# Graph kernel on one core: the second phase's inputs set up inside the last hidden products, adjacency's combinations moved from graph 0's attention to graph 1's, queries' combinations reordered

## Chip, cores and metric

The kernel runs on one core of one Trainium2 chip, in float32. The metric is the device time in microseconds, median of the timed runs. TensorE (PE) multiplies, VectorE (DVE) and ScalarE (ACT) do the elementwise work, GpSimd (POOL) does a little of it and issues stores, SyncE (SP) issues loads. Each engine works through its own instructions in program order and waits on semaphores for the others.

## The reference, cut to what matters

```python
# x: 16 graphs (B) of 1024 nodes (N) by 256 channels (C); adj: 1024 x 1024
h = max(layernorm(x), 0)
# layer 0: a graph product makes the queries, then attention of 4 heads
diff = c_adj[:, None, :] - c_adj[:, :, None]        # c_adj: mean over channels
A_s  = symmetrised abs(abs(sigmoid(diff) - 0.5) - 0.5) * 2
q    = relu(einsum('bcn,bnm->bcm', h^T, adj * A_s) * para)
k, v = split(h @ kv_w)
x    = x + softmax(q k^T * scale) v
# layer 1: aggregation with the normalised adjacency, two dense layers
h     = max(layernorm(x), 0)
A     = adj + I;  deg = column sums + row sums - diagonal of A
A_hat = A * rsqrt(deg)[:, None] * rsqrt(deg)[None, :]
y     = (A_hat @ h) @ W1.T + b1                     # 256 -> 512
y     = relu(batchnorm(y))                          # statistics over all graphs and nodes
out   = batchnorm(y @ W2.T + b2)                    # 512 -> 256
x     = x + out
```

Batch normalisation over all 16 graphs divides the kernel into two phases: no graph can be normalised before the hidden products of all of them exist.

## The kernel before

The **first phase** (`layers`) takes the graphs in turn. Attention of graph b (`attention`, 16 steps of scores, exponentials, sums and value products) is woven with a stream of other products, `background(b)`: queries (L155 by `queries`), keys and values of graph b + 1, and aggregation (`aggregate`, product pa) and hidden products (`hidden`, product py) of graph b - 1. The order is written out by hand: generators yield after each piece of about 1.71 us of TensorE, and `weave` lets side generators go on by one slot for each piece of the main one. An action given to `soon` is emitted after the next piece.

Products of 2 x 2 blocks are done with seven multiplications instead of eight, so sums and differences of blocks are needed ahead: `combine` (L415) for the normalised nodes, `take` (L455, DVE L457) for the weighted adjacency `w` in `queries`, and for A itself, once for all graphs, inside `degrees` (L209). There the transposed adjacency is loaded in eight tiles (tag `adj`, 3 buffers, shared with the loads of `adj` for the weights, L165), ScalarE sums its rows (L228), DVE takes the diagonal and adds the identity (L234 to L236), GpSimd forms the four differences (L241 to L244), and three DMAs on GpSimd's queue store the seven blocks to the DRAM tensor `aht_d` (L246 to L248). `aggregate` loads them for each graph (L600). `degrees` runs in graph 0's attention, as a side of graph 1's plain queries; `dinv`, the root of the degrees, is needed by the second norm of each graph (`shift`, L284).

`queries` runs seven products i of two pieces each. After piece 2 (`midway` of i = 1) it does `take(0,2,0,0)` and `take(0,2,0,1)`, which overwrite the right-hand blocks that product i = 2 reads. `first`, `second` and so on empty the PSUM bank of their product.

In graph b's attention the second norm of graph b - 1 (`normed`) is woven with queries from piece 9 on. Its `scale` is an rsqrt of two GpSimd instructions (L81, L82), its `shift` is on DVE. `combine("b", ...)` follows at its end.

After graph 15's attention `aggregate(15)` and `hidden(15)` run alone. Each hidden product is biased by ScalarE (L677), stored to `y1_d` by GpSimd (L678), and its statistics are taken by DVE (L681, L683).

The **second phase** (`second`) has pools of its own, opened after those of the first are closed. It loads W2 (L1078), computes the normalisation's scale and shift from the statistics, in two halves (`affine`), forms W2's combinations on GpSimd (L1091 to L1094), loads the first four inputs (`load_y`, L1101), applies relu on ScalarE (L1107) and the combinations of inputs (`combine_1` to `combine_3`), and then takes the graphs in turn: seven products m1 to m7 each (L1145), while `ahead_of` prepares the next graph's inputs. After the last graph come the second normalisation, transposes (L1263), the residual (L1269) and the output.

Of the kernel before, what the change touches and what calls it, by code (L numbers as in the profile page):

```python
# [17 lines left out]
P = 128  # L18
# [5 lines left out]
def gnn_two_layers_kernel(  # L24
# [59 lines left out]
    def layers(shifted):  # L84
# [7 lines left out]
        st = ExitStack()  # L92
        big = st.enter_context(tc.tile_pool(name=f"big_{kind}", bufs=1))
        py = st.enter_context(tc.tile_pool(name=f"py_{kind}", bufs=4))
# [4 lines left out]
        p4 = st.enter_context(tc.tile_pool(name=f"p4_{kind}", bufs=4))  # L99
        ps_sc = st.enter_context(tc.tile_pool(name=f"ps_sc_{kind}", bufs=2, space=PSUM))  # L100
# [75 lines left out]
        kvw = big.tile([P, CC, 2 * C], F32, name="kvw")  # L176
# [27 lines left out]
        deg_sm = big.tile([P, 7, NT], F32, name="deg")  # L204
        w1 = big.tile([P, CC, H1], F32, name="w1")
        dbc = big.tile([P, N], F32, name="dbc")
        row, diag, col, col_2, deg, tmp_deg, dinv = (deg_sm[:, i, :] for i in range(7))

        def degrees():  # L209

            nc.sync.dma_start(out=w1, in_=w1_t.rearrange("(k p) j -> p k j", p=P))
            nc.vector.tensor_reduce(row, rows.rearrange("p q t -> p t q"), AX.X, ALU.add)
            HT, HB = NT // 2, FB // 2
            for t in range(HT):
                for part, sums in enumerate((col, col_2)):
# [8 lines left out]
                    for n in range(2):  # L226
                        u = t + n * HT
                        nc.scalar.activation(  # L228
                            a[:, n], a[:, n], AF.Copy, accum_out=sums[:, u : u + 1]
                        )  # L230
                        if part == t * P // HB:
                            blk = a[:, n, n, t * P % HB : t * P % HB + P]
                            db = py.tile([P, P], F32, tag="y", name=f"db_{u}")
                            nc.vector.tensor_mul(db, blk, ident)  # L234
                            nc.vector.tensor_reduce(diag[:, u : u + 1], db, AX.X, ALU.add)
                            nc.vector.tensor_add(blk, blk, ident)  # L236
# [13 lines left out]
            nc.vector.tensor_add(col, col, col_2)  # L250
            nc.vector.tensor_add(deg, col, row)
            nc.vector.tensor_sub(deg, deg, diag)
            rsqrt(dinv, deg, 1.0, tmp_deg)
# [169 lines left out]
        def queries(b):  # L423
# [35 lines left out]
            def first(m):  # L459
                nc.scalar.copy(c12, m)  # L460
                nc.scalar.copy(c21, m)
                nc.vector.tensor_sub(a11, s1, a11)

            def second(m):
                add(c11, m, c12)
                nc.vector.tensor_sub(a12, a12, a11)
                soon(lambda: finish(0, 0))
# [871 lines left out]
```

## Time and profile before

| what | value |
|---|---|
| timed runs, median (range) | 2699.11 us (2698.63 to 2700.57) |
| span of the profiled execution | 2697.0 us (timed 2698.89) |
| first score product | 60.6 us |
| TensorE idle before the second phase's first product | 10.76 us, until 2418.80 |
| second phase's products | 2418.80 to 2614.9 us |
| last output transfers | 53 us, until 2680 us |

A row of waits reads: the engine and line that waited, the one that ended the wait, total us, how often, longest. A row of a timeline reads: start in us, duration, engine, line, operation, written and read tiles, shapes, count, and in brackets the idle time before and what ended it. In the kernel's names `au_f` is a tile of the transposed adjacency, `two` and `one` are the differences, `sc` scores, `p` exponentials, `o` value products.

### The profile page before, as it was taken

The numbers are of one execution on the slowest core, as the hardware profiler recorded it, in microseconds if no ns is written. First come the engines' busy times: TensorE is split into PE (matmuls) and PEld (weight loads), VectorE is DVE, ScalarE is ACT, GpSimd is POOL, SyncE is SP. The second block draws the span as 40 slices with busy tenths as digits, with TensorE's granted clock in tenths as the row PEclk, the third lists the DMA queues.
The fourth block names the chain that finished last, engine by engine and source line by source line (L and its number), as shares of the span: only waits on it lengthen the run. The fifth ranks groups of instructions, "written<-read, shape, count | busy, mean of one in ns | idle before, by whom it ended". The sixth has DMA issues, their size and how long they took to land.

```text
span 2697.0 us, 32235 instructions
## 1 busy us (share of the span) xinstructions
PE 2579.3 (96%) x11882; PEld 953.2 (35%) x11882; DVE 1742.1 (65%) x2777; ACT 1338.3 (50%) x1953; POOL 547.1 (20%) x624
## 2 busy tenths in 40 slices
PE   8689999999999999999999999999999999989994
PEld 3233333333333333333333333333333333324443
DVE  5457676666767575766666676757576665547674
ACT  5545463636454554546363645545453634335543
POOL 1341101111111111111111111111111111026653
PEclk9899999999999999999999999999999999999997
DMA  4331424242423324242424232231424233345559
GB/s 164 127 124 51 172 79 168 79 172 74 140 96 109 126 62 159 70 168 83 169 79 157 82 132 100 98 133 63 164 79 168 80 132 114 113 187 199 191 189 358
DMA packets 133606, 351.39 MB, mean 130 GB/s; under 512 B 17856, under 2 KB 38848, under 8 KB 127296
## 3 DMA queue, kind: packets, MB, share of 16 engines
q1 hardware_dynamic: 107968, 274.25, 29.0%
q0 software_dynamic: 25472, 75.00, 8.5%
q8 instruction: 96, 1.57, 0.2%
q14 instruction: 70, 0.57, 0.1%
HBM read 274.47 MB, written 74.71 MB: 129 GB/s over the span
## 4 chain that ended last, share of the span: by engine, by line
PE 79%; DVE 7%; ACT 4%; DMA 4%; issue 3%; POOL 2%; SPq 0%; POOLq 0%; DVEq 0%; ACTq 0%
PE sc L827 16%; PE o L868 16%; PE pa L155 13%; PE pg L155 9%; PE py L155 8%; PE m_f L1145 7%; PE pk L155 4%; PE pv L155 2%; PE sums L885 2%; DMA out_dram<-xo_f 2%; DVE acc L857 2%; ACT w L395 1%; PE htp L353 1%; ACT w L403 1%; DVE q L484 1%
## 5 line engine op out<-in xcount | busy, mean ns | idle before, releaser
L835 ACT ACTIVATE p<-sc 128x1024 f32<-128x1024 f32 x512 | 495.2, 1019 | 644.0 <-PE sc L827 643.1
L857 DVE TENSOR_TENSOR acc<-acc,p 128x1024 f32<-128x1024 f32 x384 | 470.9, 1226 | 154.7 <-ACT p L835 134.7
L827 PE MATMUL sc<-q,k 64*128 64x512 f32 x2048 | 514.2, 621 | 29.0 <-ACT p L835 29.0
L868 PE MATMUL o<-p,v 128*64 128x512 f32 x2048 | 497.2, 606 | 0.0
L155 PE MATMUL pg<-w,h_a 128*64 128x512 f32 x1600 | 359.7, 595 | 3.9 <-ACT k L567 2.1
L155 PE MATMUL pa<-aht,h_b 128*64 128x512 f32 x1536 | 343.5, 592 | 0.0
L827 PEld LDWEIGHTS sc<-q,k 64*128 64x128 f32 x2048 | 177.6, 187 | 351.1 <-issue 291.7
L888 POOL DMA_DIRECT2D sums_d<-row x64 | 37.2, 582 | 1051.0 <-ACT row L887 1051.0
L155 PE MATMUL py<-at,w 128*64 128x512 f32 x1024 | 230.3, 592 | 0.0
L868 PEld LDWEIGHTS o<-p,v 128*64 128x64 f32 x2048 | 124.7, 136 | 286.7 <-issue 284.4
L382 DVE SCALAR_TENSOR_TENSOR w<-w,adj 128x1024 f32<-128x1024 f32 x128 | 156.7, 1224 | 101.8 <-ACT w L403 97.8
L155 PEld LDWEIGHTS pg<-w,h_a 128*64 128x64 f32 x1600 | 115.8, 138 | 233.5 <-issue 212.4
L155 PEld LDWEIGHTS pa<-aht,h_b 128*64 128x64 f32 x1536 | 110.4, 137 | 213.2 <-issue 197.5
L677 ACT ACTIVATE y<-py,vec 128x512 f32<-128x512 f32 x128 | 87.6, 684 | 169.2 <-PE py L155 112.2
L395 ACT ACTIVATE w<-cbc,csum 128x512 f32<-128x512 f32 x256 | 170.0, 715 | 0.0
L854 DVE TENSOR_TENSOR acc<-p,p 128x1024 f32<-128x1024 f32 x64 | 78.9, 1233 | 116.2 <-ACT p L835 116.2
L678 POOL DMA_DIRECT2D y_d<-y x128 | 69.9, 546 | 343.9 <-ACT y L677 336.8
L403 ACT ACTIVATE w<-w 128x1024 f32<-128x1024 f32 x128 | 135.0, 1055 | 1.8
L457 DVE TENSOR_TENSOR w<-w,w 128x1024 f32<-128x1024 f32 x112 | 131.4, 1214 | 0.0
L155 PE MATMUL pv<-kvw,ht 128*64 128x256 f32 x1024 | 119.2, 380 | 10.6 <-DVE v L584 10.6
L893 POOL DMA_DIRECT2D inv<-sums_d x128 | 98.2, 770 | 137.6 <-DMA sums_d<-row 93.1
L681 DVE BATCH_NORM_STATS2 stats<-y 128x6 f32<-128x512 f32 x128 | 85.7, 687 | 61.5 <-ACT y L677 59.6
(155 smaller groups left out, 2840.5 us busy)
## 6 DMA issues: line engine op xcount, KB each, us to landing
aht<-aht_d SPq DMA_DIRECT2D x224, 512.0 KB, 6.1
adj<-in_adj_dram SPq DMA_DIRECT2D x128, 512.0 KB, 4.4
y_d<-y POOLq DMA_DIRECT2D x128, 256.0 KB, 2.6
yin_f<-y_d SPq DMA_DIRECT2D x32, 1024.0 KB, 6.3
x<-in_x_dram SPq DMA_DIRECT2D x32, 512.0 KB, 5.1
para<-in_para_dram SPq DMA_DIRECT2D x64, 256.0 KB, 3.9
x_d<-x POOLq DMA_DIRECT2D x16, 1024.0 KB, 10.2
xo_f<-x_d SPq DMA_DIRECT2D x32, 512.0 KB, 8.9
```

Source lines behind the costliest of these rows:

```text
L155: nc.tensor.matmul(dst[r], left[:, r], right, start=start, stop=stop)
L382: nc.vector.scalar_tensor_tensor(w, w, 1.0, a, op0=ALU.add, op1=ALU.mult)
L395: nc.scalar.activation(w[:, t, :], cbc[:, q * FB : (q + 1) * FB], AF.Abs, bias=csum[:, th * TH + t : th * TH + t + 1], scale=-1.0,)
L403: nc.scalar.activation(made[i], made[i], AF.Tanh, scale=-0.5 / C)
L457: nc.vector.tensor_sub(block(i)[part], block(x)[part], block(y)[part])
L677: nc.scalar.activation(y, made, AF.Identity, bias=b1[:, j : j + 1])
L827: nc.tensor.matmul(sc[:, e, :], ks[b][k][r, m * P : (m + 1) * P], qs[b][k][r, f * FB : (f + 1) * FB], start=True, stop=True,)
L835: nc.scalar.activation(pr, sc, AF.Exp)
L857: nc.vector.tensor_add(self.acc, self.acc, pr)
L868: nc.tensor.matmul(self.o[r, :], vs[b][k][:, m, r], pr[:, e, :], start=(m == 0), stop=(m == NT - 1),)
L893: nc.gpsimd.dma_start(out=self.inv[:, :, e], in_=sums_d[u][e].rearrange("(j q) -> q j", q=P))
L1145: nc.tensor.matmul(made, left[:, j, :], right[:, j, :], start=(j == 0), stop=(j == JH - 1))
```

## The change

Three things are done.

1. **Second phase.** `second` becomes a generator, created before `aggregate(15)` and advanced by `hidden(15)`: before the first hidden product it issues the loads of W2 and of the first two inputs and the combinations of W2; after pieces 3 to 7 it goes on with the first half of the scales, two relus, and at the end the rest of graph 0's preparation. To make room, the attention's pools (`p4`, `ps_sc`) lie on the right side and are closed after attention, and `io`, `wp` and `ps` of the second phase take their place; W2 takes the place of `kvw`, its combinations that of `dbc`, and graph 0's difference tiles that of `both`. `hidden(15)` orders its parts by j alone. The loads of inputs 2 and 3 come after graph 0's preparation.
2. **Adjacency.** `degrees` keeps loads, sums and diagonals, with loads of whole rows, and no longer stores. A new `graph()` loads the transposed adjacency again, in the old form, and does combinations and stores; it is a side of graph 1's background (4 slots in the first weave, 12 in the queries' weave, ahead of the norm). The identity is now added by GpSimd. One more key-value product precedes `columns_of(dinv)`.
3. **Queries and combine.** `take(0,2,0,0)` moves to `first`, the subtraction of a11 from `first` to `second`. `combine("b", ...)` moves from the norm's end into `aggregate`, after its first piece.

```diff
         def degrees():
             nc.sync.dma_start(out=w1, in_=w1_t.rearrange("(k p) j -> p k j", p=P))
             nc.vector.tensor_reduce(row, rows.rearrange("p q t -> p t q"), AX.X, ALU.add)
+            for t in range(NT):
+                a = load_adj_t(t, "at")
+                yield 0.0
+                blk = a[:, t * P : (t + 1) * P]
+                nc.scalar.activation(a, a, AF.Copy, accum_out=col[:, t : t + 1])
+                db = p1.tile([P, P], F32, tag="s1", name=f"db_{t}")
+                nc.vector.tensor_mul(db, blk, ident)
+                nc.vector.tensor_reduce(diag[:, t : t + 1], db, AX.X, ALU.add)
+                yield 0.0
...
+        def graph():
             HT, HB = NT // 2, FB // 2
             for t in range(HT):
-                for part, sums in enumerate((col, col_2)):
+                for part in range(2):
...
                     for n in range(2):
-                        u = t + n * HT
-                        nc.scalar.activation(
-                            a[:, n], a[:, n], AF.Copy, accum_out=sums[:, u : u + 1]
-                        )
                         if part == t * P // HB:
                             blk = a[:, n, n, t * P % HB : t * P % HB + P]
-                            db = py.tile([P, P], F32, tag="y", name=f"db_{u}")
-                            nc.vector.tensor_mul(db, blk, ident)
-                            nc.vector.tensor_reduce(diag[:, u : u + 1], db, AX.X, ALU.add)
-                            nc.vector.tensor_add(blk, blk, ident)
+                            nc.gpsimd.tensor_add(blk, blk, ident)
...
             def first(m):
                 nc.scalar.copy(c12, m)
                 nc.scalar.copy(c21, m)
-                nc.vector.tensor_sub(a11, s1, a11)
+                take(0, 2, 0, 0)
 
             def second(m):
                 add(c11, m, c12)
+                nc.vector.tensor_sub(a11, s1, a11)
                 nc.vector.tensor_sub(a12, a12, a11)
...
-                    (a12, 1, ((0, 2, 0, 0), (0, 2, 0, 1)), second),
+                    (a12, 1, ((0, 2, 0, 1),), second),
...
                     if th == NP // 2 - 1:
                         after(made)
+                    elif i == 0:
+                        combine("b", b, nc.vector)
...
             if b == B - 1:
-                parts.sort(key=lambda part: part[1] + 1.5 * part[0])
-            for g, j in parts:
+                parts.sort(key=lambda part: part[1])
+                next(turns[0])
+            for n, (g, j) in enumerate(parts):
...
                 soon(stats)
+                if b == B - 1 and n >= len(parts) // 2 - 1:
+                    soon(lambda: next(turns[0]))
...
-                yield from weave(islice(products, 4), (0, islice(w, 4)))
-                yield from weave(queries(b + 1), (0, double(w)), (9, islice(norm, 5)))
+                combined = graph() if b == 1 else iter(())
+                yield from weave(islice(products, 4), (0, islice(w, 4)), (0, islice(combined, 4)))
+                yield from weave(
+                    queries(b + 1), (0, double(w)), (0, combined), (9, islice(norm, 5))
+                )
...
-            for i in range(4):
-                load_y(i)
-            for i in range(2):
-                relu(i, 0)
+            load_y(0)
+            load_y(1)
+            yield
+            affine(0)
+            yield
+            yield
+            relu(0, 0, (0,))
+            yield
+            relu(0, 0, (1,))
+            yield
+            relu(1, 0)
             combine_1(0, nc.vector)
-            for i in (1, 0):
+            affine(1)
+            for i in (0, 1):
                 relu(i, 1)
             combine_2(0, nc.vector)
             combine_3(0)
+            load_y(2)
+            load_y(3)
+            yield
```

## The prediction

> **What bounds the kernel now.** I read the page's busy shares and slices first, then TensorE's waits over the whole span, then the busy time of the stretches where they lie, and last the queues that feed those stretches.
>
> ```profile
> PE 2579.3 (96%) x11882; PEld 953.2 (35%) x11882; DVE 1742.1 (65%) x2777; ACT 1338.3 (50%) x1953; POOL 547.1 (20%) x624
> ...
> PE   8689999999999999999999999999999999989994
> ```
>
> TensorE is busy 96%. The slices (67 us each) show less in three places: slices 1 to 3, slice 36 (2360 to 2427 us) and the output tail. TensorE's waits say who holds it up:
>
> ```profile
> PE sc L827 <- ACT p L835: 29.0, 5, 14.0
> PE m_f L1145 <- ACT yin_f L1107: 10.8, 1, 10.8
> PE pv L155 <- DVE v L584: 10.6, 14, 0.8
> PE pg L155 <- DVE w L457: 9.3, 13, 0.7
> ```
>
> Three of these four lie where the change works: 28.5 of the 29.0 us fall between 84 and 166 us (graph 0's attention), the 10.8 us are the passage into the second phase, the 9.3 us are one wait of 0.7 us in each of 13 graphs. Graph 0's attention by stretches (time, then busy us of PE, PEld, DVE, ACT, POOL, granted clock, DMA share, GB/s):
>
> ```profile
> 84.00:114.00 30.00, 14.76 (x58) 4.01 (x54) 10.15 (x30) 15.78 (x34) 14.29 (x19) 0.80 0.54 184
> 114.00:129.00 15.00, 9.20 (x32) 2.89 (x32) 2.98 (x3) 9.29 (x20) 8.67 (x13) 0.84 0.43 132
> ...
> 165.00:186.00 21.00, 21.00 (x100) 7.29 (x100) 13.91 (x22) 7.55 (x11) 15.25 (x18) 1.00 0.43 137
> ```
>
> No engine is full there, so it is a chain of waits. The chain that ended last names it: a combined adjacency block goes out, and only then the next one comes in.
>
> ```profile
> 91.31 4.29 DMA aht_d<-au_f
> 96.35 3.44 DMA au_f<-in_adj_t_dram
> 102.73 5.10 DMA aht_d<-au_f
> 108.50 3.50 DMA au_f<-in_adj_t_dram
> ```
>
> One turn takes 108.5 - 96.35 = 12.2 us. ScalarE, which must sum each block, stands before it (27.0 us over seven waits), and the exponentials queued behind the sum are what scores wait for.
>
> [...] eight score matmuls took 3.79 us after the idle 14.0 us and 1.99 us otherwise, so each long stall costs 1.8 us more. [...] the subtraction L243 takes 0.71 to 1.79 us. [...]
>
> **Part 1, adjacency's combinations leave graph 0.** From the starts of the score groups (92.68, 114.87, 129.20, 140.49, 153.69, 164.74) less the work between them at full clock (scores 1.92, outputs 1.87, sums 0.86, transposes 0.5, 1.71 for each product piece): 22.2 - 8.1, 14.3 - 7.2, 11.3 - 7.8, 13.2 - 5.5, 11.0 - 8.1, that is 14.1 + 7.1 + 3.5 + 7.7 + 2.9; and 4.9 before 92.68. Sum lost: **40.2 us**, slow clock included. The sums, the diagonals and the loads of the transposed adjacency stay (eight tiles of 512 KB), so ScalarE keeps its work; what goes is that a tile is held until its store lands. ScalarE's queue ahead of the exponentials that the 14.0 us wait is for, from 79.9: four key copies (0.57), five pairs of abs (1.33), five tanh (1.06), three sums (1.25), four relus of 0.77: 21 us, to 101; two tiles that land late add an estimated 1.6 and 2.9 (each behind a DVE product that waits for the previous sum). So scores start again at about 106.4 instead of 114.9, 5.6 us after the work ends, plus 1.8 of clock; the first 4.9 stay, and one wait of 1.3 remains. Left: 13.6. **Gain 26.6** (bounds: 34 if the loads are never late, 12 if each is).
>
> **Part 2, they go into graph 1.** No wait on TensorE is there now except 0.7 and 0.8. GpSimd then has per block four subtractions (means of L241 to L244 0.83 + 0.84 + 1.11 + 0.98) and three store issues (0.82 + 0.71 + 0.58): 5.9 us. The additions of the identity (before 0.28 on DVE) come to GpSimd, two for each of four blocks: between half of the 0.83 us of a double-sized row and all of it; I take 0.55. Eight blocks: 47.0 + 4.4 = 51.4. In its queue lie also one unit's sums (issue 0.57, wait 2.6, two issues of 1.55: 4.7) and two rsqrt of the first graph's second norm (1.10 + 2.06 and 0.57 + 1.33, mean 2.5). It starts after an inv load that now ends at 224.1. Without a wait for data the second rsqrt ends at 224.1 + 51.4 + 4.7 + 5.0 = 285.2. The first loads also wait: blocks and weights' adjacency share three buffers, four weights' tiles still have to come, so blocks 1 and 2 each wait for the store of the one before. Block 1: store issued near 229, landed 232.4, loaded 236.4, while GpSimd was free at 231: 5.4 lost; block 2 likewise 4.8. End: 295.4. Who waits: on DVE the scale of the norm (L284, now at 272.22), and behind it in order the unit's output, two accumulations and the copies of v.
>
> ```profile
> 268.92 0.13 DVE L284 TENSOR_TENSOR lnsm_b<-lnsm_b,deg 128x4 f32<-128x4 f32 x1
> ...
> 272.22 0.16 DVE L284 TENSOR_TENSOR lnsm_b<-lnsm_b,deg 128x4 f32<-128x4 f32 x1 [0.33 <-POOL lnsm_b L82]
> ...
> 277.34 1.41 DVE L584 COPY v<-pv 128x256 f32<-128x256 f32 x4
> ```
>
> The pv product that needs these copies starts at 278.2, 5.8 us after L284's second start. With 285.2 it starts at 291, with 295.4 at 301: 13 to 23 us later; I take the middle, 18, and 2 for the clock: **loss 20**. Stalls on the delayed adjacency tiles for w (estimated 5 us near 247) lie within this, since GpSimd's chain runs on meanwhile. The gather's first loads need the last store, estimated landed at 292 to 297; pa begins after pv, so this is about even. SP's para loads behind a waiting block have six pieces of slack.
>
> **Part 3, queries.** The first of the two subtractions L457 (1.22 us) moves ahead by one product, in the place of a 0.69 us subtraction that goes to `second`, both on DVE. The product waiting for it needs it at 239.3 in graph 1 and gets it at 240.0; moved, it ends near 233, eight pieces of work earlier than needed. DVE stands 0.5 us later ahead of accumulations that wait for ScalarE anyway (0.59). **Gain 9.3** (bounds 5 and 9.3). `combine` of the second norm (two of 0.69 us) moves a piece later, ahead of its first reader; nothing waited for it, 0.
>
> **Part 4, the passage.** Now the last py ends at 2408.0 (2418.80 less 10.76) and graph 1's first product starts at 2433.57: 25.6 us for 12.0 of work (28 records of 0.43). New, from T = 2408.0: w2, its combinations, the first inputs and half of the scales are ready; the weights' combinations (4 x 0.72) wait only for dbc's last reader at 2395.8. m1 runs to T + 1.7. Then the relu of input 1 (1.5 after the y at T + 0.9 and one relu), combine_1 (1.23): m5 at T + 4.5 to 6.2; the second scales at T + 5.0, relu 0.75 each: m2 to T + 8.0; relus to T + 8.1, combine_2 to T + 9.3: m6 to 11.1, then m7, m3, m4 without a wait to 16.2, and 1.8 for the clock: 18.0. **Gain 7.6** (bounds 0, if the loads don't come early, and 10). At the second py piece, at[1] is scaled at 2395.77, as the piece begins at 2395.85: 0. The tail follows unchanged, since it starts with the last statistics.
>
> **Sum** on the profiled span: 2697.0 - 26.6 + 20 - 9.3 - 7.6 = 2673.5. The timed runs stand 2.1 us above the span (2699.1), so **2675.6**.
>
> **Rivals.** (a) Graph 1 hides it all: GpSimd is busy 2 of 50 us in 200 to 250 and 10 of 50 after. Against it: DVE queues behind GpSimd's rsqrt. Loss 2 instead of 20: 2657.6. (b) Graph 0 stays bound by ScalarE's sums behind late loads: gain 12 instead of 26.6: 2690.2. For it: the 27.0 us wait is on loads; against: the chain shows stores ahead of the loads. (c) Slower: every block, not two, waits for the store before it, as nearly all did in graph 0. With 12.2 us a turn the eighth block is loaded at 218.7 + 7 x 12.2 = 304.1, combined at 313.4, rsqrt and the unit's sums bring 320, the product 326: 48 late, 2 for the clock, loss 50: 2705.6. It decides from a turn of about 11.5 us on all eight. Against: after four blocks no weights' tile is left in the three buffers. (d) The passage's loads come no earlier: 2683.2.
>
> **Chances.** Forecast (with d) 0.54, (a) 0.22, (b) 0.13, (c) 0.11. Range 2655 to 2693: from just past (a) to past (b), leaving (c) out. About 0.2% (5.4 us) is what a measurement can tell from no change: faster means under 2693.7. Faster: forecast and (a) whole, most of (b): 0.85; same 0.07 from the ends of (b) and (c); slower 0.08.
>
> **What would show it.** In graph 0: waits of scores on ScalarE below 10 us, none of SP for a store. In graph 1: GpSimd's blocks from 224 to some 290, DVE L284 waiting over 8 us for POOL, pv or pg idle near 280. L457 gone from TensorE's waits. At the passage m_f starting within 0.2 us of the last py, then gaps of 2 to 3 us. Wrong if graph 1 shows no idle TensorE, or graph 0 still more than 20 us.

## The result and the profile after

The changed kernel takes **2681.2 us** (median; 2680.35 to 2681.5) where the kernel before took 2699.09 in the same comparison (2698.63 to 2700.57). The ratio is 0.9932, 95% interval 0.9915 to 0.9949: faster by 17.9 us. The forecast was 2675.6 in a range of 2655 to 2693. The time lies inside, 5.6 us above the middle. The kernel before was timed again beside each later group of kernels, with medians of 2699.97, 2699.52 and 2700.44; the changed kernel was not, so a difference of a later kernel to it is good to about 1.4 us.

The two profiled spans, 2697.0 and 2678.6 us, can be cut at events that both kernels have. The last column is the forecast for the same stretch.

| stretch (us) | before | after | change | forecast |
|---|---|---|---|---|
| start to graph 0's first scores | 60.6 | 60.7 | +0.1 | 0 |
| graph 0: first scores to the 24 key products (pk) in a row that begin graph 1's attention | 156.6 | 131.2 | -25.5 | -26.6 |
| graph 1: those products to the first pa | 68.3 | 96.8 | +28.5 | +20 |
| first pa to the last py (queries in graphs 2 to 13) | 2122.5 | 2111.4 | -11.1 | -9.3 |
| passage: last py to graph 1's first m_f | 25.5 | 16.6 | -8.9 | -7.6 |
| second phase's products, then output | 263.4 | 261.9 | -1.6 | 0 |

So every term had the right sign, and graph 1 lost 8.5 us more than was put down for it. All that graph 0 gained was lost again in graph 1; what the kernel won in all is the queries, the passage and 1.6 us at the end.

Products are named as in the kernel: pg is a product of the queries, pk and pv of keys and values, m_f of the second phase, `sums` adds up the exponentials. Line numbers are those of the kernel that is shown, so L155 of the kernel before is L158 here.

**Page.** Busy times and TensorE's slices (67 us each) of the kernel after:

```profile
PE 2577.6 (96%) x11882; PEld 953.2 (36%) x11882; DVE 1744.0 (65%) x2768; ACT 1336.8 (50%) x1937; POOL 552.8 (21%) x632
...
PE   8897899999999999999999999999999999999994
```

Before, this row began with 8689. The 6 in slice 2 (67 to 134 us, graph 0) has become an 8, and the two 9s in slices 4 and 5 (201 to 335 us) have become a 7 and an 8: the hole has moved from graph 0 to graph 1. The 8 in slice 36 is now a 9.

**TensorE's waits** of the kernel after (total us, how often, longest):

```profile
PE pv L158 <- DVE v L591: 15.7, 14, 5.8
PE sc L841 <- ACT p L849: 11.3, 5, 5.4
PE pv L158 <- DVE q L497: 8.4, 1, 8.4
...
PE pg L158 <- DVE w L388: 4.9, 1, 4.9
```

Scores waiting for exponentials fell from 29.0 to 11.3 us. The 10.8 us of m_f for its input are gone, and short waits stand there (0.5, 1.6 and 1.5 us, shown below). The thirteen waits of pg for the subtraction in the queries are gone too. New are three single waits: 8.4 us and 5.8 us of pv, 4.9 us of pg. All three lie in graph 1, as the next views show.

**Stretches** of the kernel after (us, busy us of each engine, granted clock, DMA share, GB/s); the first two are shown of the kernel before too:

```profile
84.00:114.00 30.00, 21.85 (x92) 6.60 (x88) 10.99 (x28) 22.78 (x43) 6.52 (x7) 0.94 0.54 158
114.00:129.00 15.00, 12.23 (x54) 3.74 (x52) 8.56 (x14) 11.03 (x18) 0.00 (x0) 1.00 0.35 106
...
240.00:290.00 50.00, 32.88 (x154) 13.37 (x152) 25.23 (x51) 12.12 (x18) 31.03 (x44) 0.76 0.70 243
```

In 84 to 114 us TensorE works 21.9 instead of 14.8 us, at a clock of 0.94 instead of 0.80. The last line is the new weak stretch: 32.9 of 50 us, at a clock of 0.76, while GpSimd works 31 us of it.

**The hole in graph 1**, TensorE's timeline of the kernel after (the first line is the longest wait left of graph 0's stall):

```profile
105.47 3.62 PE L841 MATMUL sc<-q,k 64*128 64x512 f32 x8 [5.39 <-ACT p L849]
...
227.75 3.21 PE L158 MATMUL pg<-w,h_a 128*64 128x512 f32 x8 [4.89 <-DVE w L388]
...
253.02 3.78 PE L841 MATMUL sc<-q,k 64*128 64x512 f32 x8 [2.96 <-ACT p L849]
...
270.42 3.68 PE L158 MATMUL pv<-kvw_f,ht 128*64 128x256 f32 x16 [8.39 <-DVE q L497]
...
279.87 3.42 PE L158 MATMUL pv<-kvw_f,ht 128*64 128x256 f32 x16 [5.77 <-DVE v L591]
```

The last four lines are graph 1's: 22.0 us of waits, and each of the rows behind them takes 1.3 to 1.8 us longer than the same row elsewhere. What DVE did at those times, its timeline (kernel after):

```profile
226.19 1.50 DVE L388 SCALAR_TENSOR_TENSOR w<-w,adj 128x1024 f32<-128x1024 f32 x1 [7.00 <-DMA adj<-in_adj_dram]
...
265.78 0.42 DVE L290 TENSOR_TENSOR lnsm_b<-lnsm_b,deg 128x4 f32<-128x4 f32 x1 [7.56 <-POOL lnsm_b L82]
...
269.68 0.68 DVE L497 TENSOR_TENSOR q<-pg,q 128x512 f32<-128x512 f32 x1
...
273.85 0.16 DVE L290 TENSOR_TENSOR lnsm_b<-lnsm_b,deg 128x4 f32<-128x4 f32 x1 [3.49 <-POOL lnsm_b L82]
...
278.97 1.41 DVE L591 COPY v<-pv 128x256 f32<-128x256 f32 x4
```

Two pieces of work of 0.4 and 0.2 us (L290, the scale of the norm, L284 before) wait for GpSimd's rsqrt, and what TensorE needs stands in DVE's queue behind them: L497 ends 4.6 us after the first starts, and pv goes on 6.0 us after the second starts, when the first copies of v are done. GpSimd in turn (kernel after):

```profile
210.44 0.73 POOL L251 TENSOR_TENSOR two<-au_f 128x256 f32<-128x256 f32 x1 [4.96 <-DMA au_f<-in_adj_t_dram]
...
222.92 0.45 POOL L246 TENSOR_TENSOR au_f<-au_f,ident 128x128 f32<-128x128 f32 x1 [4.75 <-DMA au_f<-in_adj_t_dram]
...
235.74 0.72 POOL L251 TENSOR_TENSOR two<-au_f 128x256 f32<-128x256 f32 x1 [5.48 <-DMA au_f<-in_adj_t_dram]
...
272.78 1.04 POOL L82 TENSOR_TENSOR lnsm_b<-lnsm_b,neg_half 128x4 f32<-128x4 f32 x1
```

Blocks 1, 2 and 3 (counted from 0) wait for their loads, 15.2 us in all; the second rsqrt ends at 273.8.

The wait of 2.96 us before 253.02 has another cause. ScalarE, whose exponentials those scores need, stood still for 15.7 us (its timeline, kernel after):

```profile
251.46 0.59 ACT L901 COPY row<-sums 128x512 f32<-128x512 f32 x1 [15.71 <-DMA aht_d<-two]
```

`row`, a copy of the sums, comes from the pool `py` with its four buffers, and so do the differences `two` and `one`. It got a buffer only when the store of a `two`, issued at 247.54, had landed at 251.22. So the blocks share buffers with others in two places, not in one. This second wait doesn't decide the stretch: after it DVE still waits 7.56 us for GpSimd (265.78).

**The passage**, TensorE's timeline of the kernel after:

```profile
2394.70 5.35 PE L158 MATMUL py<-at,w 128*64 128x512 f32 x24
2399.99 1.12 PE L1164 MATMUL m_f<-yin_f,w_f 128*128 128x512 f32 x2
2401.58 1.12 PE L1164 MATMUL m_f<-yin_f,w_f 128*128 128x512 f32 x2 [0.47 <-ACT yin_f L1126]
2404.35 1.96 PE L1164 MATMUL m_f<-t_f,combined_f 128*128 128x512 f32 x4 [1.64 <-DVE t_f L1149]
2406.28 1.98 PE L1164 MATMUL m_f<-yin_f,w_f 128*128 128x512 f32 x4
2409.74 1.96 PE L1164 MATMUL m_f<-t_f,combined_f 128*128 128x512 f32 x4 [1.48 <-DVE t_f L1152]
...
2416.68 1.88 PE L1164 MATMUL m_f<-yin_f,w_f 128*128 128x512 f32 x4
```

The first m_f follows the last py without a gap; before, 10.76 us lay between. The last line is graph 1's first m_f. The chain that ended last, which before ran back into graph 0, now breaks off inside the passage, at 2404.80 us, so it says nothing on graphs 0 and 1: these had to be read from the waits and timelines above.

### The profile page after: what moved, and what is told of

Its sections match the earlier page's. It is cut to its first block, busy times and chain, and to the rows that moved or that the text cites. A ratio compares the mean times of both kernels' runs of the same rounds, so it can differ in the third digit from the quotient of the medians.

```text
span 2678.6 us, 32187 instructions
## 1 busy us (share of the span) xinstructions
PE 2577.6 (96%) x11882; PEld 953.2 (36%) x11882; DVE 1744.0 (65%) x2768; ACT 1336.8 (50%) x1937; POOL 552.8 (21%) x632
## 5 line engine op out<-in xcount | busy, mean ns | idle before, releaser
L841 PE MATMUL sc<-q,k 64*128 64x512 f32 x2048 | 512.7, 619 | 11.3 <-ACT p L849 11.3
L158 PE MATMUL pg<-w,h_a 128*64 128x512 f32 x1600 | 359.7, 594 | 10.1 <-DVE w L388 4.9
L158 PE MATMUL pa<-aht,h_b 128*64 128x512 f32 x1536 | 343.5, 592 | 0.0
L158 PE MATMUL py<-at,w 128*64 128x512 f32 x1024 | 230.4, 592 | 0.0
L388 DVE SCALAR_TENSOR_TENSOR w<-w,adj 128x1024 f32<-128x1024 f32 x128 | 157.1, 1227 | 108.2 <-ACT w L409 97.3
L158 PEld LDWEIGHTS pg<-w,h_a 128*64 128x64 f32 x1600 | 115.4, 137 | 239.5 <-issue 211.3
L158 PEld LDWEIGHTS pa<-aht,h_b 128*64 128x64 f32 x1536 | 110.3, 137 | 213.3 <-issue 198.1
L158 PE MATMUL pv<-kvw_f,ht 128*64 128x256 f32 x1024 | 122.8, 388 | 24.1 <-DVE v L591 15.7
L463 DVE TENSOR_TENSOR w<-w,w 128x1024 f32<-128x1024 f32 x112 | 134.4, 1230 | 1.5
L158 PEld LDWEIGHTS py<-at,w 128*64 128x64 f32 x1024 | 74.2, 137 | 145.2 <-issue 128.4
## 6 DMA issues: line engine op xcount, KB each, us to landing
x_d<-x POOLq DMA_DIRECT2D x16, 1024.0 KB, 10.2
```

The source lines that it names most:

```text
L158: nc.tensor.matmul(dst[r], left[:, r], right, start=start, stop=stop)
L388: nc.vector.scalar_tensor_tensor(w, w, 1.0, a, op0=ALU.add, op1=ALU.mult)
L463: nc.vector.tensor_sub(block(i)[part], block(x)[part], block(y)[part])
L841: nc.tensor.matmul(sc[:, e, :], ks[b][k][r, m * P : (m + 1) * P], qs[b][k][r, f * FB : (f + 1) * FB], start=True, stop=True,)
```

## Experiments

Theory at the start: the parts are worth what their stretches show, so the adjacency's part is a net loss, and graph 1 loses since GpSimd's long row of blocks stands ahead of a rsqrt. Rival for graph 1: the blocks are late because the three shared buffers are held until stores land. Rival for graph 0: not the buffers, but combinations and sums in one chain were what made it slow before.

Two numbers are used all through, and the expectations mean the same two ("graph 1's last key products" in them are the 24 in a row): graph 0's stretch (156.6 before, 131.2 after) and graph 1's stretch (68.3 before, 96.8 after), as defined in the table.

### 1. The three parts alone

**The adjacency's part alone** on the kernel before:

```diff
-                for part, sums in enumerate((col, col_2)):
+            for t in range(NT):
+                a = load_adj_t(t, "at")
...
+        def graph():
...
+                combined = graph() if b == 1 else iter(())
```

> Kernel before with the adjacency part alone (degrees without stores in graph 0, combinations in graph 1, one more key-value product ahead of the degrees' columns). Theory from the two profiles: graph 0's stretch (first scores to graph 1's run of 24 pk) is 25.5 us shorter, graph 1's (from there to its first pa) 28.5 us longer, of which 0.9 is won by the queries' part, so this part alone costs about 29.4 - 25.5 = +4 us: 2703 us (2699 to 2708). Rival, the forecast's own sum (-26.6 + 20): 2692.5 us. Rival, graph 1's stretch is long because of something in the other two parts: 2674 us.

Measured: 2707.7 us (before 2699.97), ratio 1.0029, interval 1.0017 to 1.0040: **7.7 us slower**. Graph 0's stretch is 130.9, graph 1's 96.7, both as in the full change. So the part is a swap: some 25 us given in graph 0, 28.5 taken in graph 1. The remainder of the 7.7 lies in two places of the profile: the passage took 28.6 instead of 25.5 (last heading), and between the first pa and the last every second graph took 0.37 longer, 2.2 in all. The latter is not in the full change, where the queries are reordered as well; its cause was not looked for.

**The queries' reordering alone** on the kernel before:

```diff
-                nc.vector.tensor_sub(a11, s1, a11)
+                take(0, 2, 0, 0)
...
-                    (a12, 1, ((0, 2, 0, 0), (0, 2, 0, 1)), second),
+                    (a12, 1, ((0, 2, 0, 1),), second),
```

> Kernel before with the queries' subtraction moved alone (take(0,2,0,0) in first, a11 in second; combine stays at the norm's end). Theory: it is the whole of the 0.93 us per graph that the two profiles differ by between one graph's first pa and the next, in 13 graphs: -12 us, 2687 us. Rival, the 0.72 us wait alone is won and the rest comes from combine: 13 x 0.72 = -9.4, 2689.7 us. Rival, the wait only moves to another product: 2699 us.

Measured: 2686.88 us, ratio 0.9951 (0.9937 to 0.9965): 13.1 us faster. From one graph to the next its pa comes 145.85 us later instead of 146.79: **0.94 us a graph**, in 13 graphs 12.2. The wait that is removed shows as 0.72 us in the trace; the other 0.2 do not show as a wait of any record. `combine` was left in its place here, and the gain per graph is the same as in the full change, so moving it is worth nothing that shows.

**The second phase's part alone** (the changed kernel with the adjacency's part, the queries' reordering and the place of `combine` put back; two of its lines, against the kernel before):

```diff
+                next(turns[0])
...
+                    soon(lambda: next(turns[0]))
```

> Changed kernel with adjacency, queries and combine put back, that is the second phase's part alone. Theory: passage from the last py to graph 1's first product 25.6 us before, 16.7 after: -8.9, 2690.2 us. The forecast had 7.6: 2691.5 us. Rival, the gain is given back in the output tail, which is bound by its transfers: 2699 us.

Measured: 2686.86 us, ratio 0.9954 (0.9940 to 0.9967): 13.1 us faster, 3.3 more than expected. The passage takes 16.6 us, as in the full change. It was 25.5 us in the profiled execution of the kernel before, but 27.7 to 28.6 in those of the two kernels above and of one below, which all have the old passage: there the second group of four products is still slow (3.75 instead of 1.96 us). The gain in the passage is thus 8.9 to 12. The end of the program is shorter as well, by 2.0 us (last heading).

**All but the adjacency's part** (the changed kernel, with combinations back in graph 0's attention):

```diff
-            for t in range(NT):
-                a = load_adj_t(t, "at")
...
-                for part in range(2):
+                for part, sums in enumerate((col, col_2)):
...
-                combined = graph() if b == 1 else iter(())
```

> Changed kernel with the adjacency part alone put back. Theory: the parts add up, adjacency costs about 4 us net, so this is faster than the changed kernel: 2699.1 - 12 - 8.9 = 2678 us (2675 to 2680). Rival, adjacency gains 6.6 net as forecast: 2688 us.

Measured: 2675.18 us, ratio 0.9908 (0.9893 to 0.9923). That is 6.0 us *faster* than the full change. Seen from both ends, the adjacency's part costs 6.0 to 7.7 us. The three parts alone add up: +7.7 - 13.1 - 13.1 = -18.5, against -17.9 measured.

### 2. What graph 1 waits for

**Buffers of their own.** The blocks take two buffers that stand free until the next graph's values fill them, instead of the three shared with the weights' adjacency:

```diff
-                    a = p3.tile([P, 2, NH, HB], F32, tag="adj", name=f"au_{kind}_{t}_{part}")
+                    a = p4.tile([P, 2, NH, HB], F32, tag="v", name=f"au_{kind}_{t}_{part}")
```

> Changed kernel, the adjacency tiles of graph() in two buffers of their own (the two of v that graph 0's values leave free) instead of the three shared with the weights' adjacency. Theory A, the chain tile - store - next load through shared buffers makes most of graph 1's loss: GpSimd's waits for tiles in blocks 1 to 3 (5.3 + 5.4 + 6.1 us) mostly go, so does TensorE's 4.9 us wait behind a late weights' tile, and the second rsqrt ends some 14 us sooner: 2681.2 - 18 = 2663 us (2659 to 2668). Theory B, the length of GpSimd's own work (51 us of combinations and store issues ahead of the norm's rsqrt) decides and the waits overlap with it: 2676 us (2673 to 2680).

Measured: 2672.98 us, ratio 0.9905 (0.9890 to 0.9920), 8.2 us better than the full change: at the lower edge of what theory B gave, 5 us above theory A. Graph 1's stretch is 88.3, and the second rsqrt ends at 265.0, 8.8 us sooner, not 14. GpSimd no longer waits for a load there, and pg no longer waits 4.9 us for late adjacency, and still the two long waits stay (TensorE's timeline of this kernel):

```profile
261.60 3.68 PE L158 MATMUL pv<-kvw_f,ht 128*64 128x256 f32 x16 [11.05 <-DVE q L497]
271.06 3.63 PE L158 MATMUL pv<-kvw_f,ht 128*64 128x256 f32 x16 [5.78 <-DVE v L591]
```

The reason is in GpSimd's timeline of this kernel, one block of the eight:

```profile
208.09 1.59 POOL L252 TENSOR_TENSOR two<-au_f,two 128x256 f32<-128x256 f32 x1
...
211.32 0.73 POOL L254 TENSOR_TENSOR one<-au_f,two 128x256 f32<-128x256 f32 x1
```

A subtraction of this size takes from 0.7 to 1.8 us, so a block takes 4.9 to 9.1 us with its stores. GpSimd's arithmetic for the eight blocks comes to 42.2 us, where it was 36.9 in the changed kernel: the time won at the loads is partly given back. In the block from 250.58 us, where DVE stood idle (248.63 to 256.96), all four subtractions took 0.72 to 0.74. Eighteen of the 32 took over 1 us. The four of these from 235 us on each overlapped a DVE operation with two inputs in SBUF: the one of 1.60 us from 240.56, for instance, one of L463 from 239.99 for 1.59 us. In the changed kernel the same is true of all twelve subtractions over 1 us (1.04 to 1.73). DVE's operations took longer beside GpSimd's there too: L388 1.50 us from 226.19, and 1.22 from 207.13, where GpSimd stood idle.

**The norm earlier.** The norm, with its two rsqrt, starts at piece 2 of graph 1's queries instead of piece 9, so that the rsqrt stand ahead of most blocks in GpSimd's queue; and both edits together:

```diff
-                    queries(b + 1), (0, double(w)), (0, combined), (9, islice(norm, 5))
+                    queries(b + 1), (0, double(w)), (0, combined), (9 if b > 1 else 2, islice(norm, 5))
```

> Changed kernel, graph 0's second norm begins at piece 2 of graph 1's queries instead of piece 9, so that its two rsqrt stand before most combinations in GpSimd's queue. Theory A (shared buffers): TensorE's 8.4 and 5.8 us waits near 270 go, since DVE no longer waits for an rsqrt behind the combinations, but the last block is stored as late as before (near 276) and the aggregation's loads wait for it instead: about 12 us come back as a wait of pa, 2674 us (2669 to 2679). Theory B (queue order alone is at fault): the whole second stall is gone and nothing replaces it, 2681.2 - 20 = 2661 us.

> Changed kernel with both: own buffers and the norm from piece 2. Theory A: chain shorter by 14 us and no rsqrt behind it; last store near 260, first use of its block near 264: 2681.2 - 25 = 2656 us (2653 to 2662). Theory B: no more than the better of the two alone.

Measured: 2676.54 us, ratio 0.9919 (0.9906 to 0.9933), with shared buffers; 2670.76, ratio 0.9895 (0.9879 to 0.9910), with buffers of their own. Graph 1's stretch is 88.5 and 86.8. The first time lies in theory A's range, but the wait of pa that was to bring back 12 us is 3.0 us, and the sums wait 9.7. The second is 2.2 us better than own buffers alone: theory A's 2656 was missed by 15 us, and theory B, no more than the better of the two, nearly held. The waits have moved rather than gone. With the norm early and shared buffers, two rows of the timeline and one of TensorE's waits:

```profile
228.98 3.68 PE L158 MATMUL pg<-w,h_a 128*64 128x512 f32 x8 [5.10 <-DVE w L388]
246.79 1.98 PE L899 MATMUL sums<-acc,ones 128*64 128x512 f32 x4 [9.73 <-DVE acc L871]
```

```profile
PE pa L158 <- DMA aht<-aht_d: 3.0, 1, 3.0
```

DVE now waits for GpSimd at an earlier place (10.72 us, until 241.38), and the accumulation for the sums stands behind it. The second group of pa products then waits 3.0 us for a block to be stored and loaded again. This lies behind the stretch, so a stretch shorter by 8.3 us brings only 4.7.

With own buffers the longest wait is another one, TensorE's and DVE's timeline:

```profile
269.35 3.68 PE L158 MATMUL pv<-kvw_f,ht 128*64 128x256 f32 x16 [7.85 <-DVE v L591]
```

```profile
268.77 1.09 DVE L591 COPY v<-pv 128x256 f32<-128x256 f32 x3 [6.38 <-issue]
```

The view names no releaser here. In the trace DVE waits on a semaphore until 268.63, and the store of the last block, issued at 265.16, landed at 268.60. The buffers called own are those of the values `v`, so a late block holds up the copies of v. That the two buffers are free is true only until then.

So another place for the norm is worth 4.7 us with the shared buffers and 2.2 with own ones. The two places tried leave the larger part of the loss, and whether arithmetic or loads make GpSimd's row long is still open here.

**Combinations in graph 0, with buffers of their own.** `graph()` runs in graph 0's attention, from the first key products on, beside the sums, and nothing of it is left in graph 1 (on top of the edit for own buffers):

```diff
                 norm, sums = Norm(2, True).all(), degrees()
+                combined = graph()
...
+                    (0, islice(combined, 4)),
...
-                yield from weave(plain_queries(1), (0, w), (0, sums), (0, norm))
+                yield from weave(plain_queries(1), (0, w), (0, sums), (0, norm), (0, combined))
```

> Changed kernel, graph() not in graph 1's but already in graph 0's attention, as a side of the first key products and of the plain queries, with the two buffers of its own. Theory: what stalled graph 0 before was not the combinations but that their tiles held the buffers that sums and weights needed; with own buffers graph 0 stays within 4 us of the changed kernel's 131 us and graph 1 returns to 67.4: 2681.2 - 29 + 4 = 2656 us (2651 to 2662). Rival: GpSimd's work beside graph 0's sums and plain queries stalls it anyway, through its queue (degrees' and norm's rsqrt) or through the transfers (4 MB more in 70 us), by 15 us or more: 2668 us or more.

Measured: **2657.76 us**, ratio 0.9846 (0.9833 to 0.9860). It beats both kernels: 23.4 us below the changed one. Graph 1's stretch is 67.4, its old length. Graph 0's is 138.0: 6.8 more than in the changed kernel, where 4 or less was expected, but with all eight blocks in it, and 16.5 to 18.7 less than in the kernels with the old order (154.5 to 156.6). So the combinations themselves were not the main reason for graph 0's stall.

### 3. Buffers against arithmetic, in both graphs

**Graph 0: only the buffers changed.** One line of the kernel before; sums, combinations and stores remain as they were. Blocks and weights then have five buffers in two places, instead of three in one:

```diff
-                    a = p3.tile([P, 2, NH, HB], F32, tag="adj", name=f"au_{kind}_{t}_{part}")
+                    a = p4.tile([P, 2, NH, HB], F32, tag="v", name=f"au_{kind}_{t}_{part}")
```

> The kernel before, with one edit: the tiles of the transposed adjacency in degrees() take two buffers of their own (those that the next graph's values fill later) instead of the three that they share with the weights' adjacency. Sums, diagonals, combinations and stores stay in graph 0's attention. Theory A (graph 0 was slow since a buffer was held until its store had landed, and not for the combinations themselves): the stretch from the first scores to graph 1's last key products falls from 154.9 to 137 to 142 us, since the kernel with the combinations in graph 0 and own buffers had 138.0; time 2681 to 2687. Theory B (sums and combinations on one chain per block are what is slow, whatever the buffers): stretch 150 to 155, time 2694 to 2700.

Measured: 2676.45 us (before 2700.44), ratio 0.9911 (0.9895 to 0.9928). Theory A, and the time is 4.5 us below its range: graph 0's stretch is **131.6**, within 0.5 us of the changed kernel, which has no combinations there at all. This one line, 24.0 us, is worth more than the whole change. The queue of loads of the kernel before, and then of this one, between 60 and 220 us (SyncE's waits; SPq is the engine's queue):

```profile
SPq L167 <- DMA aht_d<-au_f: 43.0, 4, 12.4
SPq L222 <- DMA aht_d<-au_f: 35.5, 4, 11.8
```

```profile
SPq L222 <- DMA aht_d<-au_f: 31.9, 5, 11.4
```

Before, the loads of the *weights'* adjacency (L167) also stood behind stores of combined blocks, since they shared the buffers; 78.5 us of waits in this queue have become 31.9. The longest wait of scores is 6.4 us where it was 14.0:

```profile
107.56 3.38 PE L827 MATMUL sc<-q,k 64*128 64x512 f32 x8 [6.38 <-ACT p L835]
```

**Graph 1: the arithmetic left out.** The changed kernel with GpSimd's four subtractions and the additions of the identity left out, loads and stores kept; once with the shared buffers, once with buffers of their own. The difference tiles go too, and the stores that had them read the loaded tile:

```diff
-                            nc.gpsimd.tensor_add(blk, blk, ident)
...
-                    sub(two[:, 0], b12, a[:, 0, 0])
-                    sub(two[:, 1], b22, two[:, 0])
-                    sub(b12, b22, b12)
-                    sub(one, b21, two[:, 1])
...
-                    nc.gpsimd.dma_start(out=dst[:, 4:6], in_=two)
-                    nc.gpsimd.dma_start(out=dst[:, 6], in_=one)
+                    nc.gpsimd.dma_start(out=dst[:, 4:6], in_=a[:, 0])
+                    nc.gpsimd.dma_start(out=dst[:, 6], in_=a[:, 1, 0])
```

> The changed kernel, with the four subtractions and the additions of the identity left out of graph(); loads and three stores of each block stay (the differences' places are filled from the loaded tile), so the aggregation's values are wrong and only the time is read. Theory A (graph 1 loses by the length of GpSimd's own arithmetic, which stands ahead of the norm's rsqrt): GpSimd's blocks end 30 us or more earlier, the stretch from graph 1's last key products to the first pa falls from 96.8 to 68 to 74, time 2652 to 2659. Theory B (it loses by the three shared buffers, each held until a store has landed): waits for the loads stay, 85 to 93, time 2669 to 2678. Both together would lie between.

> The same without GpSimd's arithmetic (the four subtractions and the additions of the identity left out), and with two buffers of their own for the blocks. Theory A (length of the arithmetic): no more than 2 us better than the run without own buffers, 67 to 70 us for graph 1's stretch, time 2650 to 2656. Theory B (buffers are the larger part): 10 us or more better than that run. If graph 1's stretch stays over 80 us, neither is it, and the traffic of loads and stores is left.

Measured: 2657.72 us, ratio 0.9843 (0.9827 to 0.9860), and 2650.85, ratio 0.9819 (0.9803 to 0.9836). Graph 1's stretch is 74.2 and 67.4. Both times lie in the ranges of theory A, but both theories hold in part, and the four kernels make a table of graph 1's stretch (67.4 is what it takes with nothing of the adjacency in it, in the kernel with all but the adjacency's part):

| graph 1's stretch, us | with arithmetic | without | difference |
|---|---|---|---|
| three shared buffers | 96.8 | 74.2 | 22.6 |
| two of their own | 88.3 | 67.4 | 20.9 |
| difference | 8.5 | 6.8 | |

The loss of 29.4 us is thus some 21 to 23 for GpSimd's arithmetic and 7 to 8.5 for the buffers. Two things go with the arithmetic in these runs, so the division is not exact: the wait of `row` for the store of `two` is gone too (it is not the wait that ends last in the changed kernel), and the loaded tile is held until three stores have read it, not one. That the arithmetic costs by its length, ahead of the rsqrt, is what the timelines above show; the runs don't separate it from its tiles. The loads and stores, 4 MB in and 7 MB out in these 50 us, cost nothing by themselves: without arithmetic and with free buffers the stretch is as short as without them, 67.4 us. Of the last kernel's two expectations on the buffers (at most 2 us better under A, 10 or more under B) neither came: 6.9 lies between. And GpSimd's last block was stored 21.7 us sooner, not 30. With shared buffers GpSimd waits for loads even when it has nothing to compute (its timeline, the kernel without arithmetic and with shared buffers):

```profile
210.70 0.75 POOL L244 DMA_DIRECT2D aht_d<-au_f  x1 [10.31 <-DMA au_f<-in_adj_t_dram]
...
229.40 0.75 POOL L244 DMA_DIRECT2D aht_d<-au_f  x1 [7.36 <-DMA au_f<-in_adj_t_dram]
```

A block turns round in some 9.4 us there (two turns between these lines), by waiting for the store before it and then loading; and pv still waits 4.7 us.

**Later in graph 0.** The best kernel of group 2, with the combinations starting four pieces later:

```diff
-                    (0, islice(combined, 4)),
```

> The kernel with the combinations in graph 0 and own buffers (2657.8), but starting four pieces later, with the first plain queries rather than with the first key products, so that the first transposed tiles for the sums are loaded ahead of those for the combinations. Theory A (graph 0's remaining stall of 7.7 us is from loads for the sums that stand behind loads for the combinations): the stall falls to the 5.4 us of the changed kernel and graph 0's stretch from 138.0 to 132 to 135, time 2652 to 2656. Theory B (GpSimd's length): the combinations end 8 us later and the root of the degrees with them, nothing gained, 2657 to 2664.

Measured: 2665.5 us, ratio 0.9875 (0.9858 to 0.9891), 7.7 us slower than starting at once and beyond even theory B's range. TensorE's waits from 55 to 330 us in it:

```profile
PE sc L839 <- ACT p L847: 12.8, 4, 4.8
PE cbp_deg L199 <- DVE v L591: 5.5, 1, 5.5
```

Theory A was right on its one point, that the longest wait of the scores comes from loads in each other's way: it fell from 7.7 to 4.8. But the sum over the scores' waits rose from 11.5 to 12.8, and the product that spreads the degrees now waits 5.5 us. Graph 0's stretch is 145.3 instead of 138.0. DVE's timeline says what this product waits for:

```profile
172.63 0.42 DVE L591 COPY v<-pv 128x256 f32<-128x256 f32 x1 [3.69 <-DMA aht_d<-au_f]
...
180.46 0.43 DVE L188 COPY cb_deg<-deg 128x512 f32<-128x512 f32 x1 [4.99 <-issue]
```

The values again wait for a block's store, since they lie in its buffer. `cb_deg`, from which the degrees are spread, is of the pool `py` like `two`: its wait ended at 180.42, and the store of the last `two` landed at 180.38. So the late start costs by buffers once more, not by GpSimd's length alone.

## Why the prediction was right, and where it was off

**Graph 0, gain 26.6: right, and for its reason.** Scores started again at 105.47 us after a wait of 5.39; put down were 106.4 and 5.6. The waits named as remaining were of the expected size (1.26 twice, where one of 1.3 was put down). The gain is 25.5 between the two profiles, and 23.3 to 25.5 against the other kernels that have the old graph 0 (154.5 to 156.6 us). That "what goes is that a tile is held until its store lands" is shown by the one-line experiment: the buffers alone, with every sum and combination left in place, bring 131.6. Rival (b), sums behind late loads, is out: it gave a gain of 12.

**Graph 1, loss 20: the mechanism was right, the term was mis-sized.** The chain was named as it came: blocks late for their stores, GpSimd's rsqrt behind the blocks, L290 behind the rsqrt, the copies of v behind L290, pv behind the copies. The prediction's working gave the end of the second rsqrt as 285.2 to 295.4, counted without graph 0's gain; less these 25.4 us it is 259.8 to 270.0. It ended at 273.8. pv, put at 278.2 less 25.4, or 252.8, without a delay and 13 to 23 us later with one, started at 279.87, 27.1 later. Of the 9.1 us between this and the 18 of the forecast, three steps answer:

- "I take the middle, 18": 5 us. The waits of two blocks were in the upper end, and they came; nothing spoke for half of them.
- "Blocks 1 and 2 each wait": 3.8 us. Block 3 waits too, 5.48 us, and with 1.8 us of shorter ones the waits come to 17.0 instead of 10.2. The eight blocks took some 52.6 instead of 51.4. Against this GpSimd started 2.0 us sooner (196.7 instead of 198.7), and the two rsqrt took 2.7 instead of 5.0.
- From L284's second start to pv the prediction read 5.8 us. Its own lines give 6.0 (272.22 to 278.2), and so it stayed. That and rounding are the rest.

After pv the clock brought 1.5 (3.42 us for a row of 1.90), near the 2 that were put down. The slow rows ahead of it lie inside the time that pv waits for DVE anyway, so the 6 us or so by which they are slow are no term of the sum.

"Stalls on the delayed adjacency tiles for w (estimated 5 us near 247) lie within this" was right in size and nearly in place (247 less 25.4 is 221.6; the wait of 4.89 us ended at 227.75), and right in that GpSimd's chain decided. That the buffers' part is worth 7 to 8.5 of the loss, and GpSimd's arithmetic the larger 21 to 23, agrees with how the working split it: 10.2 for waiting, the rest length. The working knew of no wait for the buffers of `two` and `one`. Rival (a), that graph 1 hides it, is out: it had a loss of 2 us, and 28.5 were measured. Rival (c) was true of three blocks out of eight, with 12.1 to 13.2 us from one block's store to the next, and did not go on after them, as was given against it: the last load of a weights' tile there was issued at 220.9 us, and from block 4 on none waits.

**Queries, gain 9.3: right, and small by 0.2 a graph.** "One wait of 0.7 us in each of 13 graphs" is 0.94 in twelve graphs; in graph 1 nothing is gained in the full change (its stretch is 96.8, and 96.7 with the adjacency's part alone). That gives 11.3; the profile shows 11.1. Alone, with thirteen graphs, it is 12.2 by that count and 13.1 by time.

**Passage, gain 7.6: right in nearly all steps.** With T the end of the last py, m1 ran to T + 2.7 instead of 1.7, after a wait of 0.47 that was not put down; it cost nothing, since m5 waits longer. m5 was put at T + 4.5 to 6.2 and ran from T + 4.3 to 6.3; m2 until T + 8.0, measured 8.2; m6 from T + 9.3, measured 9.7. The 1.8 us for the clock did not come: the rows behind the short waits take 1.96 against 1.88. Hence 16.6 instead of 18.0. The gaps were 1.6 and 1.5 us, shorter than the 2 to 3 named as a sign. Rival (d) is out, since the first input was there when the last py ended.

**The sum.** The misses are +8.5 (graph 1), +1.1 (graph 0), -1.8 (queries), -1.3 (passage), -1.6 (the end) and +0.1 (the start): 5.0 of the 5.1 by which the span, 2678.6, exceeds the 2673.5 put down; on the timed median it is 5.6. That the sum is nearer than its worst term is luck in part: three smaller misses, one of them at a place where nothing was forecast, took 4.7 us off. Of the signs, one more came short: L290's longest wait for GpSimd is 7.56 us, not over 8, though a second of 3.49 follows.

**What the profile could have told.** The chain of waits showed stores ahead of loads, and not the combinations, so own buffers could be thought of before. The forecast took the move as given, and did not ask whether the move or the buffers removed the wait. The kernels above say: the best that does all the work, 2657.76 us, has the combinations in graph 0 and gives them buffers. A further one was not tried: the kernel before with own buffers, the queries and the passage. If the gains add up, 2675.18 (all but the adjacency's part) less the 24.0 us of the buffers alone would bring it to an estimated 2651 us.

## What to carry to other kernels

When a stage stalls on a chain of store, buffer, load, first change which buffer it waits for: here one line gave 24 us, and moving the work elsewhere lost 6 to 8. Ask what else takes buffers from the same pool, now and later: `row`, `cb_deg` and the values each waited for a block's store in one of these kernels. Work moved to an engine that looks idle is charged by the first short instruction that stands behind it in that engine's queue, and by the queue of whoever waits for that (here L290, 0.42 us long, waited 7.56 us for GpSimd, and pv 8.39 us behind it); trace the order of the queue, not the share of busy time. And where a bound's two ends differ by waits that can be counted, as here, look for a reason before taking the middle: the counted end was 5 us nearer.

## What the runs showed of the hardware that was not expected

- **Two short waits of one length were answered differently.** Eight score products took 3.78 us after 2.96 us of idle (changed kernel, 253.02 us, usual 1.99), and 2.04 us after 3.00 us of idle in the one-line kernel (132.55 us). In the changed kernel the granted clock was 0.50 from 252.17 to 258.99 us, and 1.00 before and after. In the profiles of the kernels before and after, each stretch at 0.50 lasts 3.41, 6.83, 10.24, 13.65 or 17.07 us, but for the last, which the end of the trace cuts. What decides whether a short wait is followed by such a stretch is not shown.
- **A wait of 0.72 us was worth 0.94.** Removing the queries' wait moved each graph's pa by 0.94 us; the rest is in no record.
- **The old passage has two forms**, 25.5 and 27.7 to 28.6 us, in kernels whose code there is the same. In the longer form the second group of four products is slow like the first (3.75 instead of 1.96 us). In the shorter form the granted clock is 0.50 for 10.2 us there, until 2422.86, before the second group starts. The cause of the difference was not tested.
- **The tail is shorter**, by 1.6 us in the changed kernel and 2.0 with the second phase's part alone, although the change alters no step after the last product, only where the pools lie. From the end of the last transpose to the landing of the last output, which is at 2692.6 us before, it takes 27.1 us before and 24.8 after. From there to the end it is 4.4 us in both. The cause was not tested.
